# Batch 0's last four slots of row maxima, regrouped in two pairs behind the end of the first feed-forward

## The chip, the cores and the metric

The kernel runs on one core of a Trainium2 chip. The metric is the device time of one execution in microseconds (us). A core has a matrix engine (TensorE, PE in the profile, with its weight loads shown apart as PEld), a vector engine (VectorE, DVE), a scalar engine (ScalarE, ACT), GpSimd (POOL) and SyncE (SP, which here only issues DMAs). Each engine works through its own queue of instructions in order and waits on semaphores for the others. Matmuls write to PSUM, which this kernel uses as eight banks of 128 x 512 fp32.

## What is computed

A macaron block on x of 16 batches x 256 tokens x 256 features: half a feed-forward, attention, half a feed-forward, each added to x.

```python
x = x + 0.5 * _L0_ffn_ref(_layernorm(x, axis=-1), w1, b1, w2, b2)
x = x + _L0_attn_ref(_layernorm(x, axis=-1), Wq, Wk, Wv, Wo)
x = x + 0.5 * _L0_ffn_ref(_layernorm(x, axis=-1), w1, b1, w2, b2)
```

The feed-forward goes from 256 to 1024 features and back with ternary weights (-1, 0, 1, from the sizes of the given ones) and an exact GELU. The attention has 16 heads of 16 features, a rotary embedding, a causal mask and a softmax: `attn = softmax(where(causal, q @ k.T / 4, -inf))`, `out = attn @ v`, and a projection.

## The kernel before

**Staging.** There are three parts: the first feed-forward (`ffn(0, ...)`), the attention of 16 batches, and the second feed-forward (`ffn(2, ...)`). The order of work is written out by hand, and every instruction keeps its program order on its engine (all of it goes through a helper that the profile shows as line 167). So the code's order is the order of each engine's queue.

**Feed-forward.** It runs over 8 blocks of 512 tokens by 8 chunks of 128 hidden features, so 64 chunks, in 66 steps (`FFN_STEPS`). `step(u)` first issues `up` of chunk u, then `down` of chunk u - 2 (`LATE` is 2). `up` makes 4 matmuls into a single PSUM bank `m` of pool `ps_m`, two GELUs on ACT (`h_high` rounded, `h_whole` not) and their difference `h_rest` on DVE or POOL. `down` makes 8 matmuls of `h_high` and `h_rest` with `w2q` into a two-bank place `w` of pool `ps_w`, which one block holds over all its 8 chunks. With a block's last chunk, DVE adds the result to x in two operations (`x<-w,x` in the profile) and sets the place free. Steps 64 and 65 have no `up` any more, only `down` of chunks 62 and 63.

**Attention.** Each batch has 8 slots, `slot(b, p)`, of two heads each. In a slot, `scores` issues on PE the scores for the weights of batch b - 1 (`w`, keys by queries, in a two-bank place) and those for the row maxima of batch b (`m`, queries by keys). DVE then reduces the `m` scores with the mask to negative row maxima: four operations a slot (`masked<-...`, 128 or 256 columns, one for each head and half of the queries), each followed by a small read of its accumulator into `maxes`. For the weights DVE adds a mask and ACT takes the exponential into `pT`. The maxima are turned by PE (`turn_max`: transposes of `maxes`, a copy to `mT` on ACT, two DMAs from SP into rows of `qT`), so that the weights' scores of the next batch's turn come out with the maximum taken off. Other work hangs on slots: in slot 5 `turn_max(b, 0)`, which needs the maxima of slots 0 to 3; in slot 6 the transposes of a later batch (`turn_x`); from slot 1 on projections, rotations on POOL and the spread of `qT` and `kT` on ACT.

**Batch 0.** Its eight slots have maxima alone, since no batch is ahead of it; heads are taken in the order 1, 0, 3, 2, ... of pairs (`p ^ 1`), and a score's matmul contracts over the 32 rows at 32 * (head % 4). Slots 0 to 6 are issued behind steps 59 to 65 of the first feed-forward (`HEAD` is 59), slot 7 after the last step; then batch 1 follows.

**PSUM.** `ps_w` has two places of two banks, `ps_m` two of one bank, `ps_mm` two of one bank: eight in all. In batch 0 the maxima's scores are put in a `ps_w` place, because `up` uses `ps_m`; the other `ps_w` place is held by the feed-forward's last block. From batch 1 on the weights' scores use `ps_w` and the maxima's the two single banks of `ps_m`. A pool hands out the place that was given back first, and the matmuls that write to a place wait until its last reader is done.

Of the kernel before, what the change touches and what calls it, by code (L numbers as in the profile page):

```python
# [19 lines left out]
NFC = FF // P  # L20
# [9 lines left out]
def kernel(  # L30
# [19 lines left out]
    NBLK = NT // TB  # L50
# [355 lines left out]
    FFN_STEPS = NBLK * NFC + LATE  # L406
# [55 lines left out]
    def rotate(b, j, *parts):  # L462
        if 0 in parts:
            gpsimd.tensor_mul(qk[j], raw[j], cosT.unsqueeze(1).to_broadcast([P, 2, S]))
        if 1 in parts:
            gpsimd.tensor_mul(pair[j], pair[j], sinT.unsqueeze(1).to_broadcast([P, 2, S]))
        if 2 in parts:
            gpsimd.tensor_add(qk[j], qk[j], pair[j])
# [13 lines left out]
    def project_v(b, c):  # L482
        v = ps_mm.tile([P, D], FP, name="mm")
        for k in range(KC):
            tensor.matmul(
                v,
                xnT[b][:, k, c * P : (c + 1) * P],
                wv[:, k, :],
                start=(k == 0),
                stop=(k == KC - 1),  # L490
            )
        scalar.copy(vals[b % 2][:, c, :, 0:HD], v.rearrange("p (h d) -> p h d", d=HD))

    def turn_max(b, j):

        tp = ps_mm.tile([P, S], FP, name="mm")
        for c in range(2):
            tensor.transpose(tp[:, c * P : (c + 1) * P], maxes[b % 2][:, c, j, :], ident)
        mT = hp.tile([P, S], FP, name="mT")
        scalar.copy(mT, tp)  # L500
        for e in range(2):
            rows = slice(HD * (1 - e), P, 32)
            sync.dma_start(out=qT[b][rows, 2 * j + e, :], in_=mT[rows, :])

    def scores(bw, pw, bm, pm):

        w = m = None  # L510
        if bw is not None:
            w = ps_w.tile([P, 2, 512], FP, name="w")
        if bm is not None and bw is None:
            both = ps_w.tile([P, 2, 512], FP, name="w")
            m = [both[:, j, :] for j in range(2)]
        elif bm is not None:
            m = [ps_m.tile([P, 512], FP, name="m") for j in range(2)]
        for c in range(2):
            for j in range(2):
                if w is not None:  # L520
                    h = 2 * pw + j
                    rows, g = slice(32 * (h % 4), 32 * (h % 4) + 32), h // 4
                    tensor.matmul(
                        w[:, j, c * S : S + c * P],
                        kT[bw][rows, g, c * P : (c + 1) * P],
                        qT[bw][rows, g, c * P : S],
                        start=(c == 0),
                        stop=(c == 1),
                    )
                if m is not None:  # L530
                    h = 2 * pm + j
                    rows, g = slice(32 * (h % 4), 32 * (h % 4) + 32), h // 4
                    tensor.matmul(
                        m[j][:, c * P : c * P + (c + 1) * P],
                        qT[bm][rows, g, c * P : (c + 1) * P],
                        kT[bm][rows, g, 0 : (c + 1) * P],
                        start=(c == 0),
                        stop=(c == 1),
                    )
        if m is not None:  # L540
            for j in range(2):
                h = 2 * pm + j
                at = 32 * (h % 4) + HD * (1 - h // 4 % 2)
                for c in range(2):
                    cols = (c + 1) * P
                    vector.tensor_tensor_reduce(
                        out=pp.tile([P, S], FP, name="masked")[:, 0:cols],
                        in0=m[j][:, c * P : c * P + cols],
                        in1=mask_q[:, S - cols : S],
                        scale=-1.0,  # L550
                        scalar=-MASKED,
                        op0=ALU.add,
                        op1=ALU.min,
                        accum_out=maxes[bm % 2][:, c, h // 8, at : at + 1],
                    )

        def weigh():

            at = w.rearrange("p h (d w) -> p h d w", w=2 * P)[:, :, :, 0:P]
            mask = mask_k.unsqueeze(1).unsqueeze(1).to_broadcast([P, 2, 2, P])  # L560
            vector.tensor_add(at, at, mask)

            pT[bw, pw] = prp.tile([P, 2, S + P], FP, name="pT")
            scalar.activation(pT[bw, pw], w[:, :, 0 : S + P], AF.Exp, scale=HD**-0.5)

        return weigh if w is not None else lambda: None

    def attend(b, half, take=True):


        av = ps_mm.tile([P, 2, S], FP, name="mm")
        for n in range(2):
            g = 2 * half + n
            for c in range(2):
                for r in range(4):
                    tensor.matmul(
                        av[32 * r : 32 * r + 32, n, c * P : S],
                        vals[b % 2][:, c, 4 * g + r, :],
                        pT[b, 2 * g + r // 2][:, r % 2, c * S : S + c * P],
                        start=(c == 0),  # L580
                        stop=(c == 1),
                    )
        sums[b, half] = av
        if take:
            take_sums(b, half)
# [25 lines left out]
    def turn_out(b):  # L611
        tp = ps_mm.tile([P, KC, S], FP, name="mm")
        for k in range(KC):
            for c in range(2):
                tensor.transpose(
                    tp[:, k, c * P : (c + 1) * P],
                    o[b][:, c, 8 * k : 8 * k + 8, :].rearrange("p h d -> p (h d)"),
                    ident,
                )
        oT[b] = pp.tile([P, KC, S], FP, name="oT")  # L620
        scalar.copy(oT[b], tp)
# [13 lines left out]
    def add_out(b):  # L635
        at = 2 * b % BT
        xt = xs[2 * b // BT][:, at : at + 2, :]
        vector.tensor_add(xt, y_a[b], xt)

    def last_stats(b):  # L640
        for c in range(2):
            stats(2, 2 * b + c)
        finish_stats(2, 2 * b, 2)
# [7 lines left out]
    def slot(b, p, more=lambda: None):  # L651
        bw, bm = (n if 0 <= n < NB else None for n in (b - 1, b))
        up, now, past, last = (n if 0 <= n < NB else None for n in (b + 1, b, b - 1, b - 2))
        if p == 0 and 0 <= b - 3 < NB:
            add_out(b - 3)
        weigh = scores(bw, p, bm, p ^ 1)
        if p == 0 and last is not None:
            attend(last, 1)
        if p == 1 and past is not None:
            turn_max(past, 1)  # L660
        if p == 5:
            if now is not None:
                turn_max(now, 0)
            if last is not None:
                turn_out(last)
        for n, at in ((past, p + 8), (now, p)):
            slots = VALUES.get(n, (2, 6))
            if n is not None and at in slots:
                project_v(n, slots.index(at))
        if p in (1, 3) and up is not None:  # L670
            project_qk(up, p // 2)
        if p in (2, 3, 4, 5) and up is not None:
            rotate(up, p // 2 - 1, *((1, 2) if p % 2 else (0,)))
        if p == 4 and past is not None:
            attend(past, 0)
        if p == 6 and b + 2 < NB:
            turn_x(b + 2)
        if p == 7:
            if last is not None and b < NB - 1:
                project_out(last)  # L680
            if b + 3 < NB:
                ready_x(b + 3)
            if up is not None:
                spread(up, 0, 0)
        more()
        weigh()
        if p == 2 and last is not None:
            divide(last, 1)
        if p == 5 and past is not None:
            divide(past, 0)  # L690
        if p == 0 and 0 <= b - 3 < NB:
            last_stats(b - 3)

        for n, at in ((up, {7: (0, 1)}), (now, {2: (1, 0), 3: (1, 1)})):
            if n is not None and p in at:
                spread(n, *at[p])
        if b >= 1 and p % 2 == 1 and later:
            later.pop(0)()
# [19 lines left out]
    HEAD = 59  # L718
    begin, step, *_ = ffn(0, after_first)
    begin()  # L720
    for u in range(FFN_STEPS):
        step(u)
        head.get(u, lambda: None)()
        if u >= HEAD:
            slot(0, u - HEAD)
    for p in range(FFN_STEPS - HEAD, 8):
        slot(0, p)
    for b in range(1, NB - 1):
        for p in range(8):
            slot(b, p)  # L730
# [116 lines left out]
```

## Time and profile before

| what | value |
|---|---|
| median of the runs shown (623.50, 624.73, 623.47) | 623.5 us |
| the profiled execution's own time | 623.6 us |
| its span, from the first to the last instruction | 621.8 us |
| PE busy | 600.7 us, 97% |
| DVE busy | 462.1 us, 74% |
| ACT busy | 415.3 us, 67% |
| POOL busy | 306.4 us, 49% |
| mean granted TensorE clock | 0.998 |
| reductions of maxima from `m`, 128 and 256 columns | 286 and 420 ns mean, 240 each |
| reductions of maxima from `w`, 128 and 256 columns | 283 and 417 ns mean, 16 each |

The 1.8 us between the profiled execution's time and its span lie around the program. In the lists, a row has the engine, the operation, the tile written and the tiles read, partitions x elements, and how often; in a timeline it begins with start and length in us, and ends, where the engine was idle before, with how long and whose work ended that. In the trace the changed slots lie between 155 and 165 us, the first feed-forward before them and batch 1 behind them.

### The profile page before, as it was taken

To read this page: it belongs to the slowest core of one execution; us is meant where nothing else is said; L and a number is where in the kernel's file an instruction comes from. 1 tells how busy PE (TensorE), PEld (TensorE's weight loads), DVE (VectorE), ACT (ScalarE), POOL (GpSimd) and SP (SyncE) were. 2 spreads that over 40 slices of the span, in tenths; PEclk is the share of its full clock that TensorE was granted. 3 is DMA by queue.
4 is the path that set the end of the run, shared out by engine and by line. 5 is a ranking of instruction groups with operands and counts; after the bars stand their busy time and mean duration, and the time that the engine had idled before them with its cause. 6 is when DMAs were issued, how large, how long until landed. Compare 5 with 4: busy or idle time off the path is not lost.

```text
span 621.8 us, 14721 instructions
## 1 busy us (share of the span) xinstructions
PE 600.7 (97%) x5580; PEld 487.5 (78%) x5580; DVE 462.1 (74%) x1650; ACT 415.3 (67%) x716; POOL 306.4 (49%) x277
## 2 busy tenths in 40 slices
PE   4999999999999999999999999999999999999997
PEld 3798999887667777777777777777766788888886
DVE  6877777785788888888888888888885375555553
ACT  4666766674576667776777677767765666676674
POOL 3655555782464455545564456553442163334443
PEclk9999999999999999999999999999999999999999
DMA  9800000000001000110010001100100011011001
GB/s 286 178 21 1 2 1 18 17 1 18 20 35 38 18 22 35 37 36 21 19 37 36 20 20 36 37 19 21 36 4 2 1 35 35 34 35 35 26 21 56
DMA packets 25478, 21.30 MB, mean 34 GB/s; under 512 B 10944, under 2 KB 21056, under 8 KB 25408
## 3 DMA queue, kind: packets, MB, share of 16 engines
q1 hardware_dynamic: 24848, 19.44, 9.9%
q8 instruction: 44, 0.72, 0.5%
q10 hardware_dynamic: 560, 0.92, 0.4%
q14 instruction: 26, 0.21, 0.1%
HBM read 7.51 MB, written 4.19 MB: 19 GB/s over the span
## 4 chain that ended last, share of the span: by engine, by line
PE 87%; DVE 7%; ACT 2%; issue 2%; POOL 1%; DMA 1%; DVEq 0%; ACTq 0%; POOLq 0%
PE mm L167 37%; PE w L167 28%; PE m L167 21%; DVE h_rest L167 2%; DVE st L167 1%; DVE xn L167 1%; ACT h_high L167 1%; ACT h_whole L167 1%; DVE w2q L167 1%; DMA x<-in_x_dram 1%; DVE mv L167 1%; DVE masked L167 0%; DVE x L167 0%; POOL h_rest L167 0%; POOL rstd L167 0%
## 5 line engine op out<-in xcount | busy, mean ns | idle before, releaser
L167 DVE CUSTOM_DVE_ANT_0 masked<-m,mask_q 128x128 f32<-128x128 f32 x480 | 142.7, 353 | 41.0 <-PE m L167 39.7
L167 PE MATMUL m<-xnT,w1q 128*128 128x512 f32 x504 | 142.5, 404 | 0.9 <-DVE w1q L167 0.9
L167 ACT ACTIVATE h_high<-m,b_sb 128x512 fp32r<-128x512 f32 x126 | 86.7, 688 | 79.2 <-PE m L167 79.2
L167 DVE TENSOR_TENSOR h_rest<-h_whole,h_high 128x512 fp32r<-128x512 f32 x83 | 76.1, 918 | 71.0 <-ACT h_whole L167 70.6
L167 ACT ACTIVATE pT<-w 128x768 f32<-128x768 f32 x128 | 104.1, 814 | 31.6 <-DVE w L167 24.6
L167 PE MATMUL w<-qT,kT 32*128 32x256 f32 (+1 forms) x1024 | 121.7, 349 | 0.8 <-ACT pT L167 0.5
L167 POOL TENSOR_TENSOR h_rest<-h_whole,h_high 128x512 fp32r<-128x512 f32 x45 | 60.3, 1340 | 125.7 <-ACT h_whole L167 125.5
L167 PE MATMUL w<-w2q,h_high 128*128 128x256 f32 x480 | 120.9, 286 | 1.1 <-DVE w2q L167 1.1
L167 PE MATMUL w<-w2q,h_rest 128*128 128x256 f32 x480 | 118.0, 280 | 1.3 <-POOL h_rest L167 1.2
L167 PEld LDWEIGHTS w<-qT,kT 32*128 32x128 f32 x1024 | 90.7, 184 | 32.4 <-issue 26.4
L167 PE MATMUL m<-kT,qT 32*128 32x128 f32 x960 | 114.9, 349 | 0.7 <-ACT kT L167 0.7
L167 PEld LDWEIGHTS m<-xnT,w1q 128*128 128x128 f32 x504 | 86.7, 190 | 16.4 <-DVE xnT L167 2.9
L167 PEld LDWEIGHTS w<-w2q,h_rest 128*128 128x128 f32 x480 | 90.6, 189 | 6.4 <-POOL h_rest L167 1.8
L167 PEld LDWEIGHTS w<-w2q,h_high 128*128 128x128 f32 x480 | 90.4, 188 | 5.8 <-DVE w2q L167 1.6
L167 DVE TENSOR_TENSOR w<-w,mask_k 128x512 f32<-128x512 f32 x128 | 88.9, 695 | 7.1 <-PE w L167 7.1
L167 ACT ACTIVATE h_whole<-m,b_sb 128x512 f32<-128x512 f32 x126 | 85.8, 681 | 0.0
L167 PEld LDWEIGHTS m<-kT,qT 32*128 32x128 f32 x960 | 65.9, 185 | 2.9 <-ACT kT L167 1.6
L167 POOL TENSOR_TENSOR w<-w,cosT 128x512 f32<-128x512 f32 x32 | 41.2, 1289 | 51.9 <-ACT w L167 32.0
L167 PE MATMUL mm<-xnT_a,wqk 128*128 128x256 f32 x256 | 62.2, 386 | 0.0
L167 POOL TENSOR_TENSOR w<-w,sinT 128x512 f32<-128x512 f32 x32 | 40.9, 1278 | 25.7 <-DMA w<-w 25.6
L167 PEld LDWEIGHTS mm<-xnT_a,wqk 128*128 128x128 f32 x256 | 46.2, 190 | 7.6 <-issue 0.7
L167 PE MATMUL mm<-pT,vals 128*32 128x256 f32 (+1 forms) x1024 | 48.2, 329 | 0.3 <-ACT oT L167 0.3
(90 smaller groups left out, 888.0 us busy)
## 6 DMA issues: line engine op xcount, KB each, us to landing
w<-w SPq DMA_DIRECT2D x64, 128.0 KB
out_dram<-x SPq DMA_DIRECT2D x15, 256.0 KB
x<-in_x_dram SPq DMA_DIRECT2D x7, 512.0 KB
w<-in_w2T_dram SPq DMA_DIRECT2D x1, 1024.0 KB
qT<-mT SPq DMA_DIRECT2D x64, 4.0 KB
w<-in_w1T_dram SPq DMA_DIRECT2D x1, 512.0 KB
w<-in_w1T_dram ACTq DMA_DIRECT2D x1, 512.0 KB
wqk<-in_wqkvT_dram SPq DMA_DIRECT2D x16, 32.0 KB
```

Source lines behind the costliest of these rows:

```text
L167: return tc.keep_in_program_order(getattr(self.engine, name)(*args, **kwargs))
```

## The change

Slots 0 to 3 of batch 0 stay behind steps 59 to 62. Slots 4 and 5 are issued together behind step 64, slots 6 and 7 behind the last step, 65; so slot 4 goes one step later, and the rest keep their places. In slots 4 and 6 (`pm`, the pair of heads, is 5 and 7) the maxima's scores stay in a `ps_w` place; in slots 5 and 7 (`pm` is 4 and 6) they go to two single banks of `ps_m`.

```diff
@@ scores @@
-        if bm is not None and bw is None:
+        if bm is not None and bw is None and pm not in (4, 6):
             both = ps_w.tile([P, 2, 512], FP, name="w")
             m = [both[:, j, :] for j in range(2)]
         elif bm is not None:
             m = [ps_m.tile([P, 512], FP, name="m") for j in range(2)]
@@ after the first feed-forward's steps @@
     for u in range(FFN_STEPS):
         step(u)
         head.get(u, lambda: None)()
-        if u >= HEAD:
+        if u in range(HEAD, HEAD + 4):
             slot(0, u - HEAD)
-    for p in range(FFN_STEPS - HEAD, 8):
-        slot(0, p)
+
+        if u == NBLK * NFC:
+            slot(0, 4)
+            slot(0, 5)
+    slot(0, 6)
+    slot(0, 7)
     for b in range(1, NB - 1):
         for p in range(8):
             slot(b, p)
```

## The prediction

> Times are microseconds (us) from the start of the span. "Slot p" is `slot(0, p)`, one of the eight slots in which batch 0 computes its row maxima alone; "slot 1.0" is the first slot of batch 1, where weights and maxima run together. "Step u" is one step of the first feed-forward.
>
> **What bounds the kernel now.** I read the page's totals first, then the chain of waits around the place of the change, then the timeline of PE and DVE there.
>
> ```profile
> PE 600.7 (97%) x5580; PEld 487.5 (78%) x5580; DVE 462.1 (74%) x1650; ACT 415.3 (67%) x716; POOL 306.4 (49%) x277
> ```
>
> ```profile
> PE w L167 <- DVE maxes L167: 0.7, 1, 0.7
> ```
>
> ```profile
> 156.00:165.10 9.10, 8.25 (x73) 5.74 (x71) 6.67 (x35) 3.75 (x8) 6.08 (x5) 1.00 0.08 31
> ...
> 190.00:500.00 310.00, 307.99 (x3600) 235.97 (x3600) 250.40 (x1144) 216.01 (x385) 151.91 (x139) 1.00 0.07 25
> ```
>
> The first line is the page's, the second is from the list of waits of PE, the last two are stretches (length, then busy PE, PEld, DVE, ACT, POOL). PE is the bound of the whole. From 190 to 500 it idles 2.01 of 310 us; what happens before that only shifts it. In the stretch of the change PE idles 9.10 - 8.25 = 0.85 us. The change cannot make the rest of the program run quicker; it can only bring its beginning forward.
>
> ```profile
> 156.43 0.59 ACT h_whole L167
> 157.07 0.60 issue
> 157.67 0.28 DVE masked L167
> 157.96 0.34 DVE masked L167
> ...
> 158.91 0.92 PE w L167 x8
> ...
> 161.86 0.68 DVE x L167
> 162.54 0.20 DVE masked L167
> ...
> 163.70 0.69 PE w L167 x2
> ```
>
> The chain (start, length, what) leaves PE here: it runs over DVE's mask reductions and the residual add `x`. So here DVE, not PE, sets the pace.
>
> ```profile
> 155.10 0.28 PE L167 MATMUL w<-w2q,h_high 128*128 128x256 f32 x1
> ...
> 158.91 0.92 PE L167 MATMUL w<-kT,qT 32*128 32x128 f32 x8 [0.72 <-DVE maxes L167]
> ...
> 159.88 0.29 DVE L167 CUSTOM_DVE_ANT_0 masked<-w,mask_q 128x128 f32<-128x128 f32 x1 [1.03 <-PE w L167]
> ...
> 161.00 0.08 DVE L167 DVE_READ_ACCUMULATOR2_ANT maxes<- 128x1 f32 x1
> ...
> 161.25 1.29 DVE L167 SCALAR_TENSOR_TENSOR x<-w,x 128x512 f32<-128x512 f32 x2 [0.16 <-PE w L167]
> ...
> 162.46 0.28 DVE L167 CUSTOM_DVE_ANT_0 masked<-w,mask_q 128x128 f32<-128x128 f32 x1
> ...
> 164.22 0.18 PEld L167 LDWEIGHTS m<-kT,qT 32*128 32x128 f32 x1 [0.23 <-ACT kT L167]
> ...
> 164.82 0.08 DVE L167 DVE_READ_ACCUMULATOR2_ANT maxes<- 128x1 f32 x1
> ...
> 165.18 0.29 DVE L167 CUSTOM_DVE_ANT_0 masked<-m,mask_q 128x128 f32<-128x128 f32 x1 [0.27 <-PE m L167]
> ...
> 166.29 0.08 DVE L167 DVE_READ_ACCUMULATOR2_ANT maxes<- 128x1 f32 x1
> ...
> 167.18 0.29 DVE L167 CUSTOM_DVE_ANT_0 masked<-m,mask_q 128x128 f32<-128x128 f32 x1 [0.19 <-PE m L167]
> ```
>
> The reader is to see the turn: slot 5's matmuls (158.91) wait for slot 4's reductions because both use the one free two-bank place, then DVE waits 1.03 for those matmuls; 0.16 more before the residual add; 0.27 before slot 1.0's maxima at 165.18. That is 1.46 us of DVE idle between 157.67 and 165.18, and it is what can be won.
>
> **The change part by part.** Slot 4's four score matmuls move on PE from before the down-projection of step 64 to behind it; slot 5 stays behind it but writes two single banks of `ps_m`; slots 6 and 7 stay behind step 65, slot 7 in the single banks. No instruction is added or taken away. The sequences on DVE, ACT, POOL and SP keep their order, DMA issues included; only the operands of eight reductions change from `w` to `m`. Reductions cost the same from either (353 ns mean for the pair of forms from `m`; 283 and 417 ns for the two forms from `w`): 0.
>
> *When DVE can begin.* The down-projection of step 63 starts at 155.10 and its matmuls stand 0.117 apart, so eight take 0.94; the one of step 64 now follows directly at 156.04. Alone, a down-projection takes 1.03 to the next burst (155.10 to 156.13), so slot 4 starts at 157.07, 0.94 later than its 156.13 of before. Its place is free (slot 3's reductions ended at 154.4). From a burst's start to the first reduction is 0.97 (158.91 to 159.88): DVE starts slot 4 at 158.04, 0.37 later than the 157.67 of before. This is the loss in the change, and it lies on the path.
>
> *DVE's run.* Then slot 4, slot 5, the residual add, slot 6 and slot 7 need 1.20 each per slot (159.88 to 161.08) and 1.21 for the add (161.25 to 162.46): 4 x 1.20 + 1.21 = 6.01, ending at 164.05 instead of 164.90. Won: 1.03 + 0.16 of idle less the 0.37 late start, 0.82 to 0.85.
>
> *What covers the PE side.* Slot 5's banks were read last by the GELUs of step 63, done at 157.00, so it follows slot 4 at once. The two bursts take between 0.86 (eight interleaved score matmuls in slot 1.4, 176.68 to 177.54) and 2 x 0.85 (two bursts of before, 156.13 to 156.98). I take the long end: they end at 158.77, the turn of maxima (0.19) at 158.96, and the last down-projection makes the residual add possible 1.29 after its start (159.96 to 161.25), at 160.25. DVE gets there at 158.04 + 2.40 = 160.44: covered by 0.19. Slot 6 starts at 158.96 + 1.18 = 160.14, readable at 161.11, DVE wants it at 161.65. Slot 7 starts at 160.14 + 0.86 + 0.66 (turn of x) = 161.66, readable at 162.63, DVE wants it at 162.85. So all PE time in between costs nothing; the thinnest cover is 0.19, and if it is gone the excess is paid once. The DMA of the turned maxima (issued at 160.64, landed at 161.85, 2.08 after the transposes) lands by 160.85, ahead of slot 1.0.
>
> *The new wait.* Before, slot 1.0's maxima had two idle single banks and its `m` matmuls waited only for `kT` (164.22). Now slot 7 has those banks, so they wait for slot 7's reductions: the first bank at 163.45, the second at 164.05. PE reaches slot 1.0 by 162.52 and stands there about 1.5 us; behind it in PE's queue are only slot 1.0's other score matmuls and the value projection of batch 0 with ACT's copy of it, which no one needs before their 165.08 and 166.25 of now. The copy chain for `kT` (turn of x to first `m` matmul, 1.53 from 162.69 to 164.22) is over by 163.25 and hides behind it. From the release of the second bank to DVE's next reduction the nearest row is slot 1.1, which already runs so: last accumulator read ends at 166.37, next reduction at 167.18, 0.81. So DVE starts slot 1.0 at 164.05 + 0.81 = 164.86 instead of 165.18: 0.32 earlier. Bounds: with no more idle than now (0.27) it is 164.32, a gain of 0.86; with a whole new burst (0.96, 164.22 to 165.18, plus 0.06 from release to start) it is 165.07, a gain of 0.11. If PE's long end is exceeded by 0.5 after a restart, it becomes a loss of 0.4. I take 0.81, since it is the same wait, bank and engine one slot on.
>
> *Afterwards.* Slot 1.1 holds PE through the same two banks (166.37), so the 0.32 passes through it; from slot 1.2 on PE is the bound and all its feeders hang on PE: the shift is kept to the end.
>
> [...] PE shows 0.33 idle put down to issue after each short burst (at 156.98, 159.77 and 161.99). [...]
>
> Sum: -0.32 on the profiled execution (its own time 623.6, span 621.8; 0.1 above the median 623.5 of the three runs shown). Against the median: 623.5 - 0.3 = 623.2.
>
> **The rivals.**
> - *More is won (0.7 to 1.2 us, 622.3 to 622.8).* Slot 7's banks might be released early enough, bank by bank, that slot 1.0's matmuls run under slot 7's second half; then DVE's idle stays at 0.27 and the gain is 0.86. All 1.46 of DVE idle less the late start of 0.37 gives 1.09. For it: single banks are released one after the other, 0.60 apart. Against: slot 1.1 has the same early first bank and still shows 0.81.
> - *Nothing is won (623.5).* If slot 5 does not run directly behind slot 4 (the GELU of step 63 holds its bank, or its burst is late by 1.0), the reductions keep a gap and the late start eats the rest. Against: that GELU ended at 157.00.
> - *Slower (about 623.9, up to 624.8).* One mechanism: slot 1.0's burst is cut in two by the wait for slot 7's banks. Its place is between 162.5 and 165. It decides for a loss once the time from the release at 164.05 to DVE's next reduction passes 1.13 (165.18 - 164.05). A stop between the first and the second `m` bank, each with a full burst of 0.96 less the 0.60 between releases, is 0.96 + 0.36 = 1.32, a loss of 0.2; with the 0.33 issue gap twice it is about 2.0, a loss of 0.85. For it: the burst mixes `w` and `m` and PE is in order. Against: the 0.81 of slot 1.1.
>
> **How the numbers follow.** Forecast (gain of 0.1 to 0.65): 0.52. More won: 0.20, of which 0.08 for a gain over 1.25. Nothing (within 0.1): 0.12. Slower: 0.16, of which 0.08 over 1.25, where a shift would upset a meeting of queues that I cannot name. The least that a measurement here tells from no change is 0.2%, 1.25 us; the three runs before spread over that much. That gives faster 0.08, same 0.84, slower 0.08; since the sum rests on one cover of 0.19 and on one row of 0.81, I widen both ends to 0.11. The range: from the large gain (623.5 - 1.1 = 622.4) to the slower case with half its upper part (624.1), left out 0.2 together. The forecast's own range is 622.8 to 623.4.
>
> **What would show it.** Right: the 0.72 wait of PE for `maxes` at slot 5 is gone; DVE starts slot 4's reductions near 158.0 and runs without idle over 0.1 until about 164.05; a new wait on the maxima's banks stands before slot 1.0's `m` matmuls, and DVE idles near 0.8 there; PE from 190 to 500 is as busy as before. Wrong: idle on DVE between slot 5 and the residual add (the cover of 0.19 gone), slot 1.0's first reduction after 165.2, or a changed wait of PE in batches 1 to 15.

## The result, and the profile after

The changed kernel takes 626.24 us (median of 7 executions, 624.58 to 627.81), the kernel before 623.62 us beside it (623.24 to 624.73): a ratio of 1.0043, 95% interval 1.0034 to 1.0053. It is slower by 2.6 us where 0.3 us less was forecast, and outside the range of 622.4 to 624.1. The profiled execution took 625.69 us, with a span of 623.9 us (621.8 before).

The list of PE's waits of the changed kernel (total, times, longest) has the new wait; the 0.7 us that the `w` matmuls of slot 5 waited for `maxes` before is gone from it.

```profile
PE m L167 <- DVE maxes L167: 1.3, 1, 1.3
```

The timeline of PE and DVE around the change (start, length; in brackets the idle time before and whose work ended it):

```profile
156.88 0.38 PE L167 MATMUL w<-kT,qT 32*128 32x128 f32 x2
...
157.85 0.29 DVE L167 CUSTOM_DVE_ANT_0 masked<-w,mask_q 128x128 f32<-128x128 f32 x1 [0.27 <-PE m L167]
...
160.08 1.28 DVE L167 SCALAR_TENSOR_TENSOR x<-w,x 128x512 f32<-128x512 f32 x2
...
163.42 0.55 PE L167 MATMUL m<-kT,qT 32*128 32x128 f32 x1 [1.29 <-DVE maxes L167]
...
163.75 0.08 DVE L167 DVE_READ_ACCUMULATOR2_ANT maxes<- 128x1 f32 x1
...
165.15 0.29 DVE L167 CUSTOM_DVE_ANT_0 masked<-m,mask_q 128x128 f32<-128x128 f32 x1 [1.32 <-PE m L167]
...
165.46 2.08 PE L167 MATMUL mm<-wv,xnT_a 128*128 128x256 f32 x4
...
171.69 0.48 PE L167 MATMUL w<-qT,kT 32*128 32x256 f32 x1
```

The row of before for the last of these, the first matmuls of slot 1.2:

```profile
169.37 0.48 PE L167 MATMUL w<-qT,kT 32*128 32x256 f32 x1
```

Everything stands 0.18 earlier in the changed kernel already at step 63's down-projection (154.92 instead of 155.10), so a time of before is to be lowered by 0.18 in a comparison. Up to 163.83 all goes as forecast, but for 0.16 of idle on DVE ahead of slot 7's reductions: slot 4's reductions begin at 157.85 (forecast 158.04 - 0.18 = 157.86), DVE's run ends at 163.83 (163.87). Then two rows are wrong in the same way. From the release of the second bank to slot 1.0's first reduction it takes 1.32, not 0.81. And the value projection, four matmuls in 1.13 before, takes 2.08. The first matmuls of slot 1.2 come at 171.69, where the row of before gives 169.37 - 0.18 = 169.19: 2.5 us are lost between 163.8 and 171.7, by work that the change does not touch. The changed kernel, cut into stretches of 3.41 us (half of the 6.83 us for which its clock is down) counted from where the clock changes (length, then busy PE, PEld, DVE, ACT, POOL, the granted clock of TensorE as a share of full speed, DMA share, GB/s), says why:

```profile
156.54:159.95 3.41, 3.41 (x38) 2.45 (x36) 2.83 (x16) 0.66 (x2) 2.85 (x3) 1.00 0.11 40
159.95:163.36 3.41, 2.18 (x16) 1.23 (x14) 3.25 (x17) 2.37 (x5) 2.64 (x3) 1.00 0.01 4
163.36:166.78 3.42, 3.36 (x17) 2.56 (x18) 2.10 (x13) 0.00 (x0) 0.00 (x0) 0.50 0.02 5
166.78:170.19 3.41, 3.41 (x22) 2.36 (x22) 1.21 (x8) 2.59 (x4) 0.00 (x0) 0.50 0.00 0
170.19:173.60 3.41, 3.41 (x27) 2.45 (x26) 2.24 (x12) 1.44 (x3) 1.09 (x1) 1.00 0.01 5
```

The granted clock is at half from 163.36 to 170.19, 6.83 us. In the profile of before it is at full speed from 15.74 to 619.90. All 7 executions of the changed kernel have a mean clock of 0.991 to 0.997; one fall of 6.83 us makes 1 - 0.5 x 6.83 / 623.9 = 0.995, which four of them have. The page's row by slices shows it too, as the 7:

```profile
PEclk9999999999799999999999999999999999999999
```

### The profile page after: what moved, and what is told of

It is laid out like the page before. It is cut to its first block, busy times and chain, and to the rows that moved or that the text cites. A ratio compares the mean times of both kernels' runs of the same rounds, so it can differ in the third digit from the quotient of the medians.

```text
span 623.9 us, 14722 instructions
## 1 busy us (share of the span) xinstructions
PE 603.1 (97%) x5580; PEld 488.9 (78%) x5580; DVE 461.7 (74%) x1650; ACT 415.3 (67%) x716; POOL 306.2 (49%) x277
## 4 chain that ended last, share of the span: by engine, by line
PE 87%; DVE 7%; ACT 2%; issue 2%; POOL 1%; DMA 1%; DVEq 0%; ACTq 0%; POOLq 0%
PE mm L167 37%; PE w L167 28%; PE m L167 22%; DVE h_rest L167 2%; DVE st L167 1%; DVE xn L167 1%; ACT h_high L167 1%; ACT h_whole L167 1%; DVE w2q L167 1%; DVE masked L167 1%; DMA x<-in_x_dram 1%; DVE mv L167 1%; DVE x L167 0%; POOL h_rest L167 0%; POOL rstd L167 0%
## 5 line engine op out<-in xcount | busy, mean ns | idle before, releaser
L167 DVE CUSTOM_DVE_ANT_0 masked<-m,mask_q 128x128 f32<-128x128 f32 x488 | 144.9, 353 | 44.7 <-PE m L167 43.1
L167 PE MATMUL w<-qT,kT 32*128 32x256 f32 (+1 forms) x1024 | 123.3, 351 | 0.7 <-ACT pT L167 0.5
L167 PE MATMUL m<-kT,qT 32*128 32x128 f32 x976 | 118.2, 353 | 2.0 <-DVE maxes L167 1.3
L167 PEld LDWEIGHTS m<-kT,qT 32*128 32x128 f32 x976 | 67.8, 187 | 4.5 <-ACT kT L167 3.0
```

The costliest lines, as they stand in the source:

```text
L167: return tc.keep_in_program_order(getattr(self.engine, name)(*args, **kwargs))
```

## The experiments

Where the number of executions "with the full clock" is given, it is those with a mean clock of 0.998 or more. This mean does not say where an execution fell: one below it can have fallen away from the change, and only the profiled execution of each kernel has a trace that shows the place. The kernel before fell below that in 11 of 93 executions beside these runs. Each ratio is to the kernel before on the same chip; its medians there were 623.59 us (ten fillers, 32-row fillers, the projection moved, slot 5 alone), 623.34 us (four and two fillers, slot 7 alone, slot 5 with fillers) and 623.40 us (the move alone, slots 5 and 6, two places with fillers).

### Is it the clock?

In the changed kernel PE is given work in its wait, in two forms; the results of these extra matmuls are not used.

```diff
     slot(0, 6)
     slot(0, 7)
+    fill = ps_mm.tile([P, 2, S], FP, name="mm")
+    for n in range(10):
+        tensor.matmul(fill[:, 0, :], w2q[:, n % NFC, 0:P], w2q[:, (n + 1) % NFC, :], start=True, stop=True)
```

> The changed kernel with ten extra matmuls over all 128 rows (about 1.2 us, results not used) between slot 7 and slot 1.0, where PE waits 1.29 us. Theory A, the clock: PE's wait lets the granted clock fall to half from 163.4 to 170.2 us, and that alone costs the time; with PE kept at work the clock stays full and the kernel is at 623.2 us (0.4 below before). Theory B, the turn: the wait for slot 7's banks and DVE's 1.32 us of idle cost it whatever the clock is; then it stays near 626 us.

Measured: 623.00 us, ratio 0.9991 (0.9982 to 1.0000); 10 of 11 executions had the full clock. Its PE and DVE timeline:

```profile
163.41 0.34 PE L167 MATMUL m<-kT,qT 32*128 32x128 f32 x1
...
164.62 0.29 DVE L167 CUSTOM_DVE_ANT_0 masked<-m,mask_q 128x128 f32<-128x128 f32 x1 [0.80 <-PE m L167]
...
164.72 1.13 PE L167 MATMUL mm<-wv,xnT_a 128*128 128x256 f32 x4
...
168.82 0.48 PE L167 MATMUL w<-qT,kT 32*128 32x256 f32 x1
```

Here slot 4 starts at 156.88 too, and PE still cannot begin slot 1.0's `m` matmuls before 163.41: the wait for the banks is the same, and only what PE does in it differs. DVE's idle is 0.80, and slot 1.2 comes at 168.82, 2.87 us before the changed kernel's 171.69. So theory A holds and B falls: the lost time is the clock's. At 623.00 us this version is also a little faster than the kernel before, as the forecast had it for the order of work.

The second form has six matmuls over 32 rows in the same place (the line that makes `fill` is as above):

```diff
+    for n in range(6):
+        tensor.matmul(fill[:, 0, :], kT[0][0:32, 0, 0:P], kT[0][0:32, 0, :], start=True, stop=True)
```

> The same with six matmuls over 32 rows as in the scores, instead of ten over 128 rows. Theory A in the form that idle time is what counts: clock full, 623.2 us. Theory A in the form that what counts is the lack of matmuls over the whole array (between 159.1 and 165.5 us there are only transposes and scores over 32 rows): the clock falls as in the changed kernel, 626 us. Theory B: 626 us.

Measured: 625.25 us, ratio 1.0022 (1.0004 to 1.0040); 4 of 11 executions had the full clock (median 623.13), 7 had not (626.90). The profiled one took 626.90 us; its stretches around the fall:

```profile
159.00:163.40 4.40, 4.40 (x35) 3.52 (x35) 4.36 (x26) 2.22 (x6) 3.73 (x4) 1.00 0.01 2
163.40:170.20 6.80, 6.80 (x47) 5.11 (x46) 3.42 (x20) 2.50 (x5) 0.66 (x1) 0.62 0.02 4
```

PE is busy all the time before the fall, and the clock falls all the same. So idle time was not needed for this fall (PE busy for all of the 4.40 and the 6.80 us above), and what PE is given matters: with these matmuls over 32 rows 7 of 11 executions are below the full clock, with the ten over 128 rows 1 of 11. The two fillers differ in more than rows, though: `w2q` is rounded fp32 (`float32r`) and its matmuls start every 0.12 us, `kT` is plain fp32, of which each matmul of the code is two in the trace that start every 0.22 us. No run separates the rows from the type. This form also stretches PE's path somewhat (slot 7 to slot 1.0), which the medians at full clock bound to 0.15 us.

### Can useful work fill the wait?

```diff
-    VALUES = {0: (8, 10), 1: (5, 7), NB - 1: (1, 3)}
+    VALUES = {0: (7, 10), 1: (5, 7), NB - 1: (1, 3)}
```

> The changed kernel with the first value projection of batch 0 issued in slot 7 instead of slot 1.0, so that useful work of 1.06 us stands where PE waits. Theory A: clock full, 623.2 us or a little less, as slot 1.1 follows slot 1.0 at once. Theory B: 626 us.

Measured: 624.97 us, ratio 1.0019 (1.0007 to 1.0031); 3 of 12 executions had the full clock. The expectation was missed: the projection fills the wait, but its copy on ACT now stands ahead of the copies that `kT` needs (the first of them starts at 163.06 instead of 161.14), and PE waits for those instead, and after them for the reductions of slot 1.0:

```profile
164.11 0.37 PE L167 MATMUL m<-kT,qT 32*128 32x128 f32 x1 [0.73 <-ACT kT L167]
...
165.77 0.58 PE L167 MATMUL m<-kT,qT 32*128 32x128 f32 x1 [0.31 <-DVE maxes L167]
```

The stretch with little work only moved, and the clock fell at 165.63 (mean 0.66 from 163.40 to 170.20).

### Which of the two slots with single banks brings the wait?

```diff
-        if bm is not None and bw is None and pm not in (4, 6):
+        if bm is not None and bw is None and pm != 4:
```

> The changed kernel with slot 7 back in a two-bank place, so that slot 1.0's m banks are free; slot 5 keeps the single banks. Theory A: PE waits 0.5 us or less ahead of slot 1.0, the clock stays full, DVE runs through: 0.6 to 0.8 below before, 622.9 us. Theory B: the same, as the turn is gone; if it is slower than before, neither is right and slot 4's and 5's regrouping has a cost of its own.

Measured: 622.58 us, ratio 0.9986 (0.9977 to 0.9994); 8 of 11 executions had the full clock (median 622.43, 1.15 under the 623.58 of the kernel before with full clock, where 0.6 to 0.8 was expected). Slot 7's matmuls now wait for the residual add, and slot 1.0's need not wait for the banks at all:

```profile
161.74 0.92 PE L167 MATMUL w<-kT,qT 32*128 32x128 f32 x8 [0.89 <-DVE x L167]
...
162.75 0.48 PE L167 MATMUL w<-qT,kT 32*128 32x256 f32 x1
...
168.17 0.48 PE L167 MATMUL w<-qT,kT 32*128 32x256 f32 x1
```

Then slot 7's single banks were put into the kernel before, with nothing moved:

```diff
-        if bm is not None and bw is None:
+        if bm is not None and bw is None and pm != 6:
```

> The kernel before with one edit: slot 7 alone uses the two single banks; nothing is moved. This is the new wait by itself. The wait for slot 7's banks puts DVE's first reduction of slot 1.0 at 164.9 + 0.8 = 165.7 instead of 165.2: 0.5 slower at full clock, 624.1; with theory C the window from 161.2 on loses the scores of slot 1.0 and the clock falls in part of the executions, up to 626.5.

Measured: 625.52 us, ratio 1.0035 (1.0021 to 1.0049). 3 of 11 executions had the full clock, at 623.83 (median), 0.5 over the 623.33 of the kernel before with full clock; 8 had not, at 626.77. So this edit alone brings both the small loss that the wait costs in order and the large one of the clock.

The move alone, with every slot in a two-bank place:

```diff
-        if bm is not None and bw is None and pm not in (4, 6):
+        if bm is not None and bw is None:
```

> The move alone: slots 4 and 5 behind step 64, slots 6 and 7 behind step 65, all of them in two-bank places as before. Slot 5's matmuls wait for slot 4's reductions (end near 159.2), so its reductions start near 160.2, 0.3 later than before, and the rest follows: 0.3 slower at full clock, 623.7 us. Theory C: slot 1.0 keeps its free single banks, but PE stands about 1.1 us ahead of slot 5, between two down-projections full of work: no window gets poor and the clock stays.

Measured: 626.31 us, ratio 1.0038 (1.0020 to 1.0056); 4 of 12 executions had the full clock (623.73, as expected for the order), 8 had not (627.36). The expectation that the clock would stay was wrong. In the profiled execution PE's wait ahead of slot 5 was enough, though it stands between two down-projections:

```profile
159.46 1.34 PE L167 MATMUL w<-kT,qT 32*128 32x128 f32 x8 [1.30 <-DVE maxes L167]
```

Its clock fell at 159.83, right behind this wait, for about 3.4 us: the mean is 0.61 from 159.00 to 163.40, so (1 - 0.61) x 4.40 / 0.5 = 3.43, and 1.00 from there to 170.20. So slot 7's single banks alone and the move alone are each slower than the kernel before, and the move with slot 5's single banks is faster.

### How much work holds the clock?

To size it I counted, per window of 3.41 us (the length of the fall in the move alone, and half of that in the changed kernel), the columns of all matmuls that start in it, each weighted by the share of the array's rows that it uses (32 of 128 rows is a quarter; the sum is in units of one column over all 128 rows). The window and the weight are choices of mine, to be judged by how they order the runs. The groups of PE in the changed kernel's window from 159.95 to 163.36 (PE's idle falls in it):

```profile
L167 PE MATMUL w<-qT,kT 32*128 32x256 f32 x2 | 0.7, 412 | 0.0
L167 PE MATMUL mm<-ident,xn_a 128*128 128x128 f32 x4 | 0.7, 286 | 0.0
L167 PE MATMUL m<-kT,qT 32*128 32x256 f32 x4 | 0.6, 376 | 0.0
L167 PE MATMUL m<-kT,qT 32*128 32x128 f32 x4 | 0.5, 321 | 0.0
L167 PE MATMUL w<-kT,qT 32*128 32x256 f32 x2 | 0.4, 374 | 0.0
```

That is 2 x 256 / 4 + 4 x 128 + 4 x 256 / 4 + 4 x 128 / 4 + 2 x 256 / 4 = 1152 units (1024 if the last row, which begins ahead of the window, is left out). Such a window of before, 162.51 to 165.92, holds 2176. With four filling matmuls over 128 rows instead of ten, and then with two (`range(2)`):

```diff
-    for n in range(10):
+    for n in range(4):
```

> The changed kernel with only four extra matmuls over 128 rows (about 0.5 us) ahead of slot 1.0, so that some 0.8 us of PE's wait stays idle. Theory C, array work per window: the clock is decided in windows of 3.41 us by how much of the array's columns and rows is used, and falls where a window has about 1536 column units or less (a column unit: one column streamed through all 128 x 128 cells; the changed kernel's window had 1024, and one with 32-row filler had 1536 with PE never idle). Four matmuls add 1024, so every window stays above: clock full, 623.0 us. Theory D, idle time: 0.8 us idle is more than with ten matmuls (0), and the clock still falls in most executions: 625 us or more.

Measured: 624.93 us, ratio 1.0019 (1.0005 to 1.0032); 4 of 12 executions had the full clock (622.82), 8 had not (625.79).

> The same with two extra matmuls (0.25 us, 512 units). Theory C: windows of 1024 to 1536 units remain at many phases, so the clock falls in many executions but not all: median between 623.5 and 626. Theory D: falls as in the changed kernel, 626.

Measured: 625.84 us, ratio 1.0024 (1.0009 to 1.0039); 3 of 12 executions had the full clock (622.85), 9 had not (625.95).

Theory C's threshold of about 1536 was too low: the profiled execution with four matmuls fell after a window with 1792, and a second time at 468.48, far from the change. But idle time (D) does not order the runs either. By work added to the wait, executions below the full clock are 7 of 7 (0 units), 9 of 12 (512), 7 of 11 (768, the 32-row filler: its six matmuls of the code are twelve in the trace, 12 x 256 / 4), 8 of 12 (1024) and 1 of 11 (2560). The three in the middle are too close to be told apart with so few executions. What does stand out is that the 32-row filler leaves PE without idle, as the ten matmuls do, and falls like the fillers that leave some. The profiled executions with two and four matmuls are ordered neither by idle nor by the count: with two PE still waited 0.9 for `maxes`, its window held 1664 units, and the clock stayed full; with four PE waited 0.6, the window held 1792, and the clock fell. Over all 13 profiled executions the clock fell ten times ahead of the program's end, after windows of 1024 to 2176 units; windows from 1600 up have also kept it, none below 1600 has, and none above 2176 fell. So the count is a help and no more: what decides between 1600 and 2176 no run shows. Two simpler counts do worse. Columns without the weight for rows: the fall with the 32-row filler follows a window of 6144, and windows of 3328 kept the clock. Units without the transposes by `ident`: windows of 768 kept it.

### Further versions

Slot 5 alone in single banks, with four filling matmuls where PE waits 0.89 ahead of slot 7 (against the version with slot 5 alone):

```diff
     slot(0, 6)
+    fill = ps_mm.tile([P, 2, S], FP, name="mm")
+    for n in range(4):
+        tensor.matmul(fill[:, 0, :], w2q[:, n % NFC, 0:P], w2q[:, (n + 1) % NFC, :], start=True, stop=True)
     slot(0, 7)
```

> The version with slot 5 alone in single banks (622.58 us, with a fall of the clock in some executions) and four extra 128-row matmuls where PE waits 0.89 us ahead of slot 7. Theory C: the fills cost nothing, as they lie in the wait, and the falls around 160 us go: 622.4 us and fewer executions over 623. Theory D says the same here; if it is slower than 622.6, the fills are not hidden.

Measured: 622.19 us, ratio 0.9983 (0.9973 to 0.9992); 9 of 12 executions had the full clock (622.10). The profiled one had not (623.57): its clock fell at 466.78, far from the change, and was full around 160. The version without the filler was full there too in its profiled execution, so that the filler removes falls is not shown; that it costs nothing is: at full clock the two versions are 1.23 and 1.15 us under the kernel before on their chips.

Slots 5 and 6 in single banks instead of slots 5 and 7:

```diff
-        if bm is not None and bw is None and pm not in (4, 6):
+        if bm is not None and bw is None and pm not in (4, 7):
```

> The changed kernel with the single banks given to slots 5 and 6 instead of 5 and 7: slot 1.0's banks are then free one slot earlier, and slot 7's place does not wait for the residual add. The same as slot 5 alone at full clock (622.2 to 622.6), as DVE's run sets both; PE's wait is now ahead of slot 6. Falls of the clock about as often as with slot 5 alone.

Measured: 623.15 us, ratio 1.0001 (0.9986 to 1.0016); 6 of 12 executions had the full clock (622.52, as expected), 6 had not (625.10). Its median is that of the kernel before. It was below the full clock oftener than slot 5 alone (3 of 11), but counts this small do not decide whether the expectation on the falls holds. The profiled execution fell twice, at 162.19 and at 469.39.

And the version with four fills, with four more ahead of batch 2, where PE waits for `kT`:

```diff
     for b in range(1, NB - 1):
         for p in range(8):
+            if (b, p) == (2, 0):
+                fill = ps_mm.tile([P, 2, S], FP, name="mm")
+                for n in range(4):
+                    tensor.matmul(fill[:, 0, :], w2q[:, n, 0:P], w2q[:, n + 1, :], start=True, stop=True)
             slot(b, p)
```

> The version with slot 5 alone in single banks and four 128-row matmuls ahead of slot 7, and four more between batch 1's last slot and batch 2's first, where PE waits 0.7 us for kT and the windows are the next poorest (1600 to 1900 units). Theory C: the falls there go too and the fills hide in the wait: median 622.2, fewer executions over 623. If PE's wait there is not idle all through, up to 0.3 slower.

Measured: 622.09 us (621.94 to 622.18), ratio 0.9974 (0.9964 to 0.9985); all 7 executions had the full clock. It has the lowest median of the study; its interval overlaps that of the version with one filler (0.9973 to 0.9992). Its PE timeline shows both fillers inside the waits:

```profile
160.30 0.71 PE L167 MATMUL mm<-w2q 128*128 128x256 f32 x4
161.43 0.93 PE L167 MATMUL w<-kT,qT 32*128 32x128 f32 x8 [0.42 <-DVE x L167]
...
181.87 0.82 PE L167 MATMUL mm<-w2q 128*128 128x256 f32 x4
183.57 0.37 PE L167 MATMUL m<-kT,qT 32*128 32x128 f32 x1 [0.26 <-ACT kT L167]
```

That seven executions never fell may be luck: the version with one filler was below the full clock in 3 of 12, which these counts do not tell from none of 7, and a further window with little work, 1664 units from 462.81 on, is untouched.

## Why the prediction was wrong, point by point

- *When DVE can begin* and *DVE's run*: right. 157.85 and 163.83 against 157.86 and 163.87 (shifted by the 0.18), with 0.16 of idle ahead of slot 7 that the prediction did not have.
- *What covers the PE side*: right that it is all hidden; the pair of bursts took 0.88 (156.88 to the transposes at 157.76), the short end of the range, not the long one. The residual add followed slot 5's reductions at once.
- *The new wait*: its place was right (slot 1.0's `m` matmuls wait for slot 7's reductions), and so was its price at full clock: 0.80 of idle on DVE in the version with ten fillers, against 0.81. The wait on PE was 1.29 by the profile, for about 1.5.
- **The step that failed** is in the same paragraph: "PE reaches slot 1.0 by 162.52 and stands there about 1.5 us; behind it in PE's queue are only" matmuls that nobody needs earlier. PE's standing was priced at nothing beyond its own length. It has a second price: behind a stretch with little work on the array TensorE's clock was at half for 3.41 us (the move alone) or 6.83 us (the changed kernel), and here PE is the bound as soon as slot 1.2 is reached. From 163.4 to slot 1.2 this cost 2.87 us, against the 0.32 that the order was to gain. That the loss is the clock's is shown by the ten fillers, and by the version with two, whose executions take 622.85 us with the full clock and 625.95 without; which amount of work lets the clock fall stays open.
- *Afterwards*, "the 0.32 passes through": right at full clock, as far as the versions with fillers show it; the changed kernel itself had no execution with the full clock. Slot 1.2 begins at 168.82 in the version with ten fillers, 0.37 before the 169.19 of before; in executions with full clock the whole is 622.98 against 623.58, 0.60 less. What makes up the rest of the 0.60 was not followed.
- *The rivals*: the slower one named the place and the wait (the burst of slot 1.0, between 162.5 and 165), but its mechanism, full bursts and issue gaps, did not occur at full clock, and its upper figure, 624.8, is still 1.4 under the result. Its 1.32 from the release to the next reduction is what the changed kernel's trace shows, but by luck: at full clock it is 0.80. The rows shown could not warn, as the clock is 1.00 in all of them; what could have been asked is why one of the three runs of before took 624.73.
- *The 0.33 of idle put down to issue*, one behind each short burst: in the changed kernel it stands once behind the pair, at 157.76. The shorter burst of the pair bought nothing, as DVE set the pace (1.20 a slot, 162.63 to 163.83 for slot 7, against 0.88 for two slots on PE), and could only make the wait of PE longer.

The 3.41 us before the fall of the changed kernel were not idle ones: PE was busy for 2.18 of them, and a wait of 1.29 was enough. In the 32-row filler no wait was needed.

## What to carry to other kernels

Before PE is left to wait, or put on fp32 matmuls over few rows, count the array work in every 3.4 us around that place. Ahead of the program's end, no window above 2176 units lost the full clock in these traces, and none below 1600 kept it; where it falls, the price is that of the half clock (here 2.87 us), not the length of the wait. A wait that moves from one place to another is not neutral even where the order gains (the changed kernel: 0.60 less at full clock, with the ten fillers, and 2.6 more without them). Where a stretch with little work can't be avoided, full-size matmuls without use, inside the wait, can keep what the order gains: ten of them brought the changed kernel from 626.24 to 623.00 us, while four or two left most executions below the full clock.

## What the runs showed of the hardware that I had not expected

- Two falls stand at regular distances. The traces show the full clock first at 16.59 us in the changed kernel and at 15.74 in the kernel before (four `m<-xnT,w1q` matmuls that take 2.04 us at 11.67 and 11.86 take 1.09 and 1.10 from 19.08 and 19.29 on). The fall of the changed kernel comes 163.36 - 16.59 = 146.77 us after that and lasts 6.83, the one at the end of the kernel before comes 619.90 - 15.74 = 604.16 after: 43, 2 and 177 times 3.413. As the first full clock does not come at the same time in both, a fall at such distances need not meet the same place of the program. That may be why one kernel has executions with and without a fall (622.85 and 625.95 us, medians, in the version with two fillers); it is not shown, as each kernel has one trace.
- A busy PE did not hold the clock by itself: with the filler of plain fp32 over 32 rows PE is busy all through 159.00 to 170.20, and the clock falls at 165.09. Ten matmuls of rounded fp32 over 128 rows held it in 10 of 11 executions.
- The kernel before is below the full clock too, in 11 of 93 executions. Where it falls no trace shows; three of the versions fall between 466.78 and 469.39, far from all that was changed.
- What the clock follows stays open: by my count of units falls follow windows of up to 2176, and windows of 1600 have kept it.
